# Attention and float8 layer on one core: queries and keys projected three slots ahead of their scores, the float8 product moved within the chunk

## The chip, the core and the metric

The kernel runs on one core of one Trainium2 chip. A core has TensorE (PE; its weight loads are shown apart as PEld), VectorE (DVE), ScalarE (ACT), GpSimd (POOL) and SyncE (SP), which here only issues DMAs. The metric is the device time of one execution in microseconds (us). The kernel before took 2824.32 us, the median of four runs (2822.94 to 2827.62).

## The reference, cut to what matters

The input is x of (4, 1024, 512): four sequences of 1024 tokens. There are 16 heads of 128.

```python
xn = layernorm(x)
q  = rope(rmsnorm(xn @ Wq + bq))            # 16 heads x 128
lk = rope(rmsnorm(xn @ Wlk + blk));  lv = xn @ Wlv + blv
w  = softmax over each 4 tokens of (xn @ Wcmp + bcmp)
entries = sum over the 4 tokens of w * xn   # 256 per sequence
ck = rope(rmsnorm(entries @ Wk + bk));  cv = entries @ Wv + bv
sparse = softmax of the 8 largest q @ ck.T (causal), times cv
local  = softmax of q @ lk.T over a window of 128 back, times lv
out = x + (sparse + local) / 2 @ Wo + bo + fp8(xn) @ fp8(input2)
```

## The kernel before, in words

The 4096 tokens are cut into 32 chunks of 128. A chunk has eight units, a unit is two heads of one chunk, so there are 256 units. All weights stay in SBUF once they are loaded. The main loop (from L785) goes over slots s = -2 to 257. A slot is software-pipelined over several units, and all engines' instructions are written out by hand in the order in which the loop calls them; nothing reorders them. `place(s)` gives the chunk t and the unit u of 0 to 7.

In slot s, for the unit named:

- `scores` (L570 to L581): q times the keys of the previous and the present chunk (lkT) and times the compressed keys (ckT), into PSUM `sc`.
- `weigh` (L603 to L618): VectorE masks, finds the maxima and the eight largest; ScalarE takes exponents. `settle` (L625 to L636) normalises the sparse part, `settle_window` (L641) the window.
- `queries` of unit s + 2 (L443, L444): one product for q and lk of both heads, 128x512 in `qp`.
- `squares`, `spread` (L294, L288, L289): ScalarE sums squares, GpSimd makes the factor `r`. `normalize` (L465, then `rotate`, L307 to L310): VectorE scales into `th`, and VectorE and GpSimd (`rb`) apply the rotation.
- For units from 8 on, `turn_keys` and `fetch_keys` (L510 to L528) turn q and lk: VectorE transposes 32x32 blocks into `thb`, four DMAs write `qk` to DRAM, two DMAs read it back as `qT` and `lkT`. All of these are in SP's queue. Units 0 to 7 are turned by TensorE (`turn_keys_here`, `keep_keys`, L488 to L495).
- `turn` and `fetch` (L659 to L701) do the same for the probabilities of unit s: `probB`, `pr` in DRAM, `probT`.
- `values_of` (L535): lv of unit s + 1, into `vp`; `keep_values` (L547) copies it on ScalarE.
- `values` (L718): context of unit s - 1 from probT, lv and cv. `keep_context` (L733), `to_output` (L751): unit s - 2 into the output.

Work of a chunk is cut into steps of generators, and the loop advances every running generator twice a slot by `steps()`, after `settle` and after `to_output` is called. `chunk_prep(t + 2)` starts at u = 7 and makes the layer norm (`bn_stats` at u = 7, `xn` at 0, transposes `xp` at 1), the compressed entries (`yp` at 2, `ep` at 4, `kv` at 4 to 6) and at u = 7 of the next chunk the transpose `cp` (L410) and VectorE's copy into `ckT` (L412). `chunk_eight(t)` starts at u = 3: three VectorE instructions and four of GpSimd round xn to float8 (L261 to L272), at u = 5 TensorE multiplies (`fp`, L423) and VectorE and GpSimd add the result (`f`, L428, L429).

The PSUM pool tag `pp` has two buffers of 128x512. xp, yp, ep, cp, fp, vp, the transposes of the first units and a few constants share them. The tag `scratch` in SBUF has three buffers for xn, y, qv, qm, f and a mask.

Of the kernel before, what the change touches and what calls it, by code (L numbers as in the profile page):

```python
# [12 lines left out]
F32 = mybir.dt.float32  # L13
# [6 lines left out]
P = 128  # L20
# [4 lines left out]
BLK = 32  # L25
NB = P // BLK
# [12 lines left out]
def kernel(  # L39
# [26 lines left out]
    nc = tc.nc  # L66
# [4 lines left out]
    NU = NH // 2  # L71
    NE = P // RATIO
    NT = B * NCH
    NN = NT * NU
# [3 lines left out]
    work = ctx.enter_context(tc.tile_pool(name="work", bufs=2))  # L78
# [5 lines left out]
        return v.rearrange("p (b i) -> p b i", i=BLK)  # L84

    def scratch(name, shape=(P, 512), dtype=F32):
        return work.tile(list(shape), dtype, tag="scratch", name=name, bufs=3)

    def pp(name):
        return psum.tile([P, 512], F32, tag="pp", name=name, bufs=2)  # L90
# [7 lines left out]
    def load_x(t, purpose):  # L98

        b, c = divmod(t, NCH)  # L100
        xt = work.tile([P, HID], F32, tag="x", name=f"x_{purpose}_{t}")
        nc.sync.dma_start(xt, hidden[b, ts(c, P), :])
        x_tiles[purpose, t] = xt
# [15 lines left out]
    wo_sb = [const.tile([P, 2, HID], F32, name=f"wo_{u}") for u in range(NU)]  # L119

    def load_wqk(u, engine):
        for i, w in enumerate((Wq, Wlk)):
            engine.dma_start(
                wqk_sb[u][:, :, ts(i, 256)], w[:, ts(u, 256)].rearrange("(k p) n -> p k n", p=P)
            )
# [41 lines left out]
    scales = const.tile([P, 2], F32, name="scales")  # L167
# [77 lines left out]
    def late_constants():  # L245

        nc.scalar.dma_start(bo_sb, bo.partition_broadcast(P))
        nc.vector.tensor_tensor(inv, scales[:, 0:1], scales[:, 1:2], ALU.mult)
        nc.vector.reciprocal(inv, inv)

        bp = pp("blvT_ps")
        nc.tensor.transpose(bp[:, 0:NH], blv_n, ident[:NH, :NH])
        nc.scalar.activation(blvT, bp[:, 0:NH], AF.Copy, scale=0.5)

    def quantize(dst, src, scalar, tag):

        v = scratch(f"qv_{tag}") if tag[0] == "x" else src
        m = scratch(f"qm_{tag}")  # L260
        nc.vector.tensor_scalar(v, src, scalar, None, ALU.mult)  # L261
        nc.vector.tensor_scalar(
            m.bitcast(U32), v.bitcast(U32), 0x7F800000, None, ALU.bitwise_and
        )
        nc.vector.tensor_scalar(m, m, FP8_MIN_NORMAL, 1.5 * 2.0**20, ALU.max, ALU.mult)
        nc.gpsimd.tensor_tensor(v, v, m, ALU.add)
        yield
        nc.gpsimd.tensor_tensor(v, v, m, ALU.subtract)
        yield
        nc.gpsimd.tensor_scalar(m, v, FP8_OVERFLOW, 0.0, ALU.mult, ALU.mult)  # L270
        yield
        nc.gpsimd.tensor_tensor(dst, v, m, ALU.add)  # L272
        yield

    w2_sb = const.tile([P, KK, HID], BF16, name="w2_sb")


    w2_raw = [wo_sb[NU // 2 + k][:, 0, :] for k in range(KK)]

    def round_w2():  # L280
        for k in range(KK):
            yield from quantize(w2_sb[:, k, :], w2_raw[k], scales[:, 1:2], f"w2_{k}")

    def rstd_of(ss, n, mul, eps, name):

# [129 lines left out]
    def chunk_eight(t):  # L415

        xt, xnT = x_tiles["sum", t], chunks[t]
        x8 = work.tile([P, KK * P], BF16, tag="x8", name=f"x8_{t}", bufs=1)
        src = xnT.rearrange("p k s -> p (k s)")
        yield from quantize(x8, src, scales[:, 0:1], f"x_{t}")  # L420
        fp = pp(f"fp_{t}")
        for k in range(KK):
            nc.tensor.matmul(  # L423
                fp, x8[:, ts(k, P)], w2_sb[:, k, :], start=(k == 0), stop=(k == KK - 1)
            )
        yield
        f = scratch(f"f_{t}")
        nc.vector.scalar_tensor_tensor(f, fp, inv, bo_sb, ALU.mult, ALU.add)  # L428
        nc.gpsimd.tensor_tensor(xt, xt, f, ALU.add)  # L429
# [4 lines left out]
    def place(n):  # L434

        return divmod(n, NU)
# [41 lines left out]
    def by_dma(n):  # L478

        return NU <= n < NN - 1  # L480
# [15 lines left out]

    def key_tiles(n):
        w = units[n]
        qT = work.tile([P, NB, 2 * BLK], F32, tag="qT", name=f"qT_{n}")
        lkT = work.tile([P, NB, 2 * BLK], F32, tag="lkT", name=f"lkT_{n}", bufs=NU + 2)  # L500
        w["qT"], w["lkT"] = qT.rearrange("p a (i g) -> p (a i) g", g=2), lkT
        return qT, lkT

# [148 lines left out]
    def turn(n):  # L652
        parts = parts_of(n)
        g = len(parts)
        pb = work.tile([P, 1024], F32, tag="probB", name=f"probB_{n}", bufs=1)
        pb = of_heads(pb, n)
        for h in range(2):
            prob = heads.pop((n, h))["prob"]
            nc.vector.transpose(  # L659
                pb[:, :, ds(h * g, g), :],  # L660
                prob[:, parts[0] * P : (parts[-1] + 1) * P].rearrange(
                    "p (g b i) -> p b g i", b=NB, i=BLK
                ),
            )
        turned = dram.tile([P, 1024], F32, tag="pr", name=f"pr_{n}")
        turned = turned[:, 0 : NB * 2 * g * BLK]
        nc.sync.dma_start(turned, pb.rearrange("p b g i -> p (b g i)"))
        units[n]["pr"] = turned
# [27 lines left out]
    def fetch(n):  # L696
        probT = work.tile([P, 1024], F32, tag="probT", name=f"probT_{n}", bufs=1)
        probT = of_heads(probT, n)
        turned = units[n].pop("pr").rearrange("(a j) (b x) -> b j a x", a=NB, b=NB)
        for b in range(NB):  # L700
            nc.sync.dma_start(  # L701
                probT[ds(b * BLK, BLK)].rearrange("j a g i -> j a (g i)"), turned[b]
            )
        units[n]["probT"] = probT
# [61 lines left out]
    def steps(n=1):  # L766
        for g in running:
            for _ in range(n):
                next(g, None)

    def until(g, step):
        for at in g:
            if at == step:
                break

    def for_unit(n, *todo):
        if 0 <= n < NN:
            for f, *more in todo:
                f(n, *more)

    first, rounding = chunk_prep(0), round_w2()
# [4 lines left out]
    pick_tokens()  # L786
    masks()

    for s in range(-2, NN + 2):
        t, u = place(s)  # L790

        if s == -2 or u == 7 and 0 <= t and t + 2 < NT:
            running = [*running[-2:], chunk_prep(t + 2)]
        if u == 3 and 0 <= t < NT:
            load_x(t, "sum")
            running = [*running[-2:], chunk_eight(t)]
        if u == 4 and 0 <= t and t + 2 < NT:
            load_x(t + 2, "norm")

        for_unit(s, (scores, 0), (scores, 1))  # L800
        for_unit(s - 2, (keep_context,))
        for_unit(s, (weigh, 0), (weigh, 1))
        for_unit(s + 2, (queries,))
        if not by_dma(s + 1) and s < NU:
            for_unit(s + 1, (turn_keys_here,))
        for_unit(s, (settle, 0), (settle, 1))
        if s < 0:
            until(first, "B4" if s == -2 else "B6")
        steps()
        for_unit(s + 2, (squares, (0, 1, 2, 3)), (spread,))  # L810
        if not by_dma(s + 1) and s < NU:
            for_unit(s + 1, (keep_keys,))
        for_unit(s, (settle_window, 0), (settle_window, 1))
        for_unit(s - 2, (to_output,))
        steps()
        if by_dma(s):
            turn(s)
        if s == -1:
            until(first, "B7")
        for_unit(s + 1, (values_of,))  # L820
        if s == -1:
            until(first, "B8")
        if not by_dma(s):
            for_unit(s, (turn_here,))
        for_unit(s + 2, (normalize,))
        for_unit(s - 1, (values,))
        if by_dma(s):
            fetch(s)
        else:
            for_unit(s, (keep_turned,))  # L830
        if s + 2 >= NU:
            for_unit(s + 2, (turn_keys,), (fetch_keys,))
        for_unit(s + 1, (keep_values,))
        if s < NU:

            if s == -1:
                late_constants()
                for k in range(KK):
                    nc.scalar.dma_start(w2_raw[k], input2[ts(k, P), :])
            if 0 <= s < KK:  # L840
                for _ in range(4):
                    next(rounding, None)
            if 3 <= s + 5 < NU:
                load_wqk(s + 5, nc.scalar)
            if 3 <= s + 4 < NU:
                load_wlv(s + 4, nc.scalar)
            if 0 <= s + 1 < NU:
                load_wo(s + 1, nc.scalar)
        if u == 6 and 0 <= t and t + 2 < NT:
            load_angles(t + 2)  # L850
        units.pop(s - 1 - NU, None)
# [46 lines left out]
```

## Time and profile before

| | |
|---|---|
| median of four runs | 2824.32 us |
| the profiled execution | 2824.67 us |
| its span, first to last instruction | 2822.9 us |
| granted TensorE clock, mean | 0.998 |
| VectorE busy | 81% |
| ScalarE busy | 46% |
| GpSimd busy | 29% |
| DMA, mean over the span | 142 GB/s |

The page comes from one profiled execution. Busy shares are over the whole span. A group's line names the line of code, the engine, what it writes and reads, the count, the busy time and the mean of one in ns, then the engine's idle time before it and who ended it. In the timeline each row has its start, its length, engine, line and tiles, and rows of the same kind that follow each other are merged. A slot takes 9.0 to 12.7 us, more with later chunks of a sequence (more compressed keys) and in slots with steps of a chunk: the medians in the last chunk of a sequence are 10.92, 11.36, 12.66, 10.92, 11.67, 11.78, 10.92 and 11.29 us for u = 0 to 7.

### The profile page before, as it was taken

To read this page: it belongs to the slowest core of one execution; us is meant where nothing else is said; L and a number is where in the kernel's file an instruction comes from. 1 tells how busy PE (TensorE), PEld (TensorE's weight loads), DVE (VectorE), ACT (ScalarE), POOL (GpSimd) and SP (SyncE) were. 2 spreads that over 40 slices of the span, in tenths; PEclk is the share of its full clock that TensorE was granted. 3 is DMA by queue.
4 is the path that set the end of the run, shared out by engine and by line. 5 is a ranking of instruction groups with operands and counts; after the bars stand their busy time and mean duration, and the time that the engine had idled before them with its cause. 6 is when DMAs were issued, how large, how long until landed. Compare 5 with 4: busy or idle time off the path is not lost. (4 is left out here: it accounts for less than half of the span.)

```text
span 2822.9 us, 48528 instructions
## 1 busy us (share of the span) xinstructions
PE 2769.5 (98%) x12770; PEld 1875.8 (66%) x12969; DVE 2278.4 (81%) x9132; ACT 1300.5 (46%) x5075; POOL 816.6 (29%) x1161
## 2 busy tenths in 40 slices
PE   7999999999999999999999999999999999999998
PEld 4666666666666666666666666666666666666765
DVE  5778888888878888888877788888887777888886
ACT  3444444444444444444444444444444444444443
POOL 3433222322233332232223233222223222322222
PEclk9999999999999999999999999999999999999999
DMA  7344445555444445555544444555554444455554
GB/s 223 95 140 133 135 142 153 149 151 147 137 124 134 139 133 148 149 153 150 148 129 124 136 133 140 150 152 146 152 146 124 132 129 135 136 152 149 150 147 121
DMA packets 620851, 399.85 MB, mean 142 GB/s; under 512 B 306880, under 2 KB 573984, under 8 KB 620576
## 3 DMA queue, kind: packets, MB, share of 16 engines
q1 hardware_dynamic: 608352, 383.18, 48.0%
q10 hardware_dynamic: 12224, 13.56, 1.5%
q8 instruction: 105, 1.72, 0.3%
q14 instruction: 170, 1.39, 0.2%
HBM read 212.53 MB, written 184.03 MB: 140 GB/s over the span
## 5 line engine op out<-in xcount | busy, mean ns | idle before, releaser
L443 PE MATMUL qp<-wqk,xnT 128*128 128x512 f32 x2048 | 944.3, 604 | 3.5 <-DMA scales<-in_L_ffn_scale_dram 2.7
L443 PEld LDWEIGHTS qp<-wqk,xnT 128*128 128x128 f32 x2048 | 370.1, 191 | 383.0 <-issue 369.8
L610 ACT ACTIVATE prob<-sc,neg 128x256 f32<-128x256 f32 (+1 forms) x512 | 235.6, 460 | 791.2 <-DVE taken L609 777.3
L535 PEld LDWEIGHTS vp<-wlv,xnT 128*128 128x128 f32 x2048 | 390.6, 191 | 171.2 <-issue 108.6
L535 PE MATMUL vp<-wlv,xnT 128*128 128x256 f32 x2048 | 487.5, 381 | 7.3 <-DVE lkT L495 4.1
L751 PE MATMUL op<-wo,cT 128*128 128x512 f32 x1024 | 488.1, 599 | 6.0 <-ACT cT L733 1.5
L659 DVE STREAM_TRANSPOSE probB<-prob 128x512 f32<-128x512 f32 (+2 forms) x494 | 282.9, 610 | 76.6 <-ACT prob L641 73.0
L294 ACT ACTIVATE junk<-qp 128x128 bf16<-128x128 f32 x1024 | 283.6, 277 | 96.1 <-remote 53.1
L307 POOL TENSOR_TENSOR rb<-th,cs 128x256 f32<-128x256 f32 x256 | 247.1, 965 | 276.7 <-DVE th L465 276.7
L465 DVE SCALAR_TENSOR_TENSOR th<-qp,r,norm_w 128x128 f32<-128x128 f32 x1024 | 283.1, 339 | 45.8 <-POOL r L289 45.5
L751 PEld LDWEIGHTS op<-wo,cT 128*128 128x128 f32 x1024 | 186.5, 190 | 179.2 <-issue 116.4
L547 ACT COPY lv<-vp 128x256 f32<-128x256 f32 x256 | 95.3, 372 | 450.3 <-PE cp L718 395.7
L288 POOL TENSOR_SCALAR r<-ss 128x4 f32<-128x4 f32 x256 | 49.5, 193 | 861.6 <-ACT junk L294 855.1
L718 PE MATMUL cp<-probT,lv 128*128 128x128 f32 x1920 | 297.5, 275 | 0.6 <-DMA probT<-pr 0.6
L718 PEld LDWEIGHTS cp<-probT,lv 128*128 128x128 f32 x1920 | 274.4, 191 | 14.1 <-PE vp L535 0.9
L289 POOL TENSOR_TENSOR r<-r,nhalf 128x4 f32<-128x4 f32 x256 | 259.6, 1014 | 21.3
L718 PE MATMUL cp<-probT,cv 128*128 128x128 f32 x1536 | 255.1, 275 | 0.0
L580 PE MATMUL sc<-ckT,qT 128*128 128x96 f32 (+7 forms) x1024 | 226.1, 303 | 0.0
L641 ACT ACTIVATE prob<-prob,tot 128x256 f32<-128x256 f32 (+1 forms) x512 | 222.8, 484 | 2.4 <-DVE tot L635 2.4
L309 DVE TENSOR_TENSOR th<-thb,rb 128x128 f32<-128x128 f32 x256 | 87.2, 341 | 158.5 <-POOL rb L307 158.5
L577 PE MATMUL sc<-lkT,qT 128*128 128x128 f32 x1024 | 208.9, 286 | 6.2 <-DMA lkT<-qk 4.4
L718 PEld LDWEIGHTS cp<-probT,cv 128*128 128x128 f32 x1536 | 212.7, 192 | 0.0
(123 smaller groups left out, 4002.6 us busy)
## 6 DMA issues: line engine op xcount, KB each, us to landing
pr<-probB SPq DMA_DIRECT2D x127, 512.0 KB, 2.6
probT<-pr SPq DMA_DIRECT2D x508, 128.0 KB, 2.9
qk<-thb SPq DMA_DIRECT2D x992, 64.0 KB, 2.0
pr<-probB SPq DMA_DIRECT2D x96, 384.0 KB, 2.3
probT<-pr SPq DMA_DIRECT2D x384, 96.0 KB, 2.4
qT<-qk SPq DMA_DIRECT2D x248, 128.0 KB, 2.3
lkT<-qk SPq DMA_DIRECT2D x248, 128.0 KB, 2.6
x_norm<-_attn_hidden_states_dram SPq DMA_DIRECT2D x32, 256.0 KB, 3.0
```

What stands on the lines that cost most here:

```text
L289: nc.gpsimd.tensor_tensor(r, r, nhalf[: ss.shape[0], 0:n], ALU.pow)
L294: nc.scalar.activation(junk[: src.shape[0]], src, AF.Square, accum_out=acc)
L307: nc.gpsimd.tensor_tensor(bb, x12, wide(cs[:, HALF:ROPE]), ALU.mult)
L443: nc.tensor.matmul(qp, xnT[:, k, :], wqk_sb[u][:, k, :], start=(k == 0), stop=False)
L465: nc.vector.scalar_tensor_tensor(th[:, i, :], qp[:, ts(i, D)], r[:, i : i + 1], norm_w[:, i // 2, :], ALU.mult, ALU.mult,)
L535: nc.tensor.matmul(vp[:, 0:256], xnT[:, k, :], wlv_sb[u][:, k, :], start=(k == 0), stop=(k == KK - 1),)
L580: nc.tensor.matmul(sc[:, spa], q, ckT[:, 0:m], start=True, stop=False)
L610: nc.scalar.activation(prob[:, loc], sc[:, loc], AF.Exp, bias=neg[:, 0:1], scale=-1.0, accum_out=tot[:, 0:1],)
L641: nc.scalar.mul(prob[:, loc], prob[:, loc], tot[:, 0:1])
L659: nc.vector.transpose(pb[:, :, ds(h * g, g), :], prob[:, parts[0] * P : (parts[-1] + 1) * P].rearrange("p (g b i) -> p b g i", b=NB, i=BLK),)
L718: nc.tensor.matmul(blocks(cp[:, h, :]), v, probT[:, :, h * len(parts) + i - parts[0], :], start=(i == parts[0]), stop=(i == parts[-1]),)
L751: nc.tensor.matmul(op, cT[:, h, :], wo_sb[u][:, h, :], start=(u == 0 and h == 0), stop=(u == NU - 1 and h == 1),)
```

## The change

- Queries, their squares, factors and normalisation are those of unit s + 3 instead of s + 2; the loop starts at s = -3. TensorE's turning of the first eight units' keys is that of s + 2 instead of s + 1, the turning through DRAM that of s + 3. qT has three buffers, lkT one more. The loads of wqk go out a slot earlier.
- `scratch` has two buffers instead of three. Rounding input2 at the start uses a half of a tile of wo, which is loaded later, as its scratch.
- `chunk_eight(t)` starts at u = 5 instead of 3, so that its product stands at u = 7 instead of 5.

```diff
-        return work.tile(list(shape), dtype, tag="scratch", name=name, bufs=3)
+        return work.tile(list(shape), dtype, tag="scratch", name=name, bufs=2)
...
-    def quantize(dst, src, scalar, tag):
+    def quantize(dst, src, scalar, tag, m=None):
...
-        m = scratch(f"qm_{tag}")
+        if m is None:
+            m = scratch(f"qm_{tag}")
...
-            yield from quantize(w2_sb[:, k, :], w2_raw[k], scales[:, 1:2], f"w2_{k}")
+            spare = wo_sb[NU // 2 + k][:, 1, :]
+            yield from quantize(w2_sb[:, k, :], w2_raw[k], scales[:, 1:2], f"w2_{k}", spare)
...
-        qT = work.tile([P, NB, 2 * BLK], F32, tag="qT", name=f"qT_{n}")
-        lkT = work.tile([P, NB, 2 * BLK], F32, tag="lkT", name=f"lkT_{n}", bufs=NU + 2)
+        qT = work.tile([P, NB, 2 * BLK], F32, tag="qT", name=f"qT_{n}", bufs=3)
+        lkT = work.tile([P, NB, 2 * BLK], F32, tag="lkT", name=f"lkT_{n}", bufs=NU + 3)
...
-    for s in range(-2, NN + 2):
+    for s in range(-3, NN + 2):
...
             load_x(t, "sum")
+        if u == 5 and 0 <= t < NT:
             running = [*running[-2:], chunk_eight(t)]
...
-        for_unit(s + 2, (queries,))
-        if not by_dma(s + 1) and s < NU:
-            for_unit(s + 1, (turn_keys_here,))
+        for_unit(s + 3, (queries,))
+        if s + 2 < NU:
+            for_unit(s + 2, (turn_keys_here,))
...
-            until(first, "B4" if s == -2 else "B6")
+            until(first, ("B3", "B4", "B6")[s + 3])
...
-        for_unit(s + 2, (squares, (0, 1, 2, 3)), (spread,))
-        if not by_dma(s + 1) and s < NU:
-            for_unit(s + 1, (keep_keys,))
+        for_unit(s + 3, (squares, (0, 1, 2, 3)), (spread,))
+        if s + 2 < NU:
+            for_unit(s + 2, (keep_keys,))
...
-        for_unit(s + 2, (normalize,))
+        for_unit(s + 3, (normalize,))
...
-        if s + 2 >= NU:
-            for_unit(s + 2, (turn_keys,), (fetch_keys,))
+        if s + 3 >= NU:
+            for_unit(s + 3, (turn_keys,), (fetch_keys,))
...
-            if 3 <= s + 5 < NU:
-                load_wqk(s + 5, nc.scalar)
+            if 3 <= s + 6 < NU:
+                load_wqk(s + 6, nc.scalar)
```

## The prediction, before the result

> **What bounds the kernel now.** I read the page's engine shares first, then PE's waits, then the timeline around one chunk.
>
> ```profile
> PE 2769.5 (98%) x12770; PEld 1875.8 (66%) x12969; DVE 2278.4 (81%) x9132; ACT 1300.5 (46%) x5075; POOL 816.6 (29%) x1161
> ```
>
> TensorE is busy 98% of the span: 53.4 us of 2822.9 are idle, and some 33 of these lie before the first scores (15.6), in the first and last chunk (7.4 and 5.7) and after the last product (4.1). No edit here removes TensorE work, so a gain can only come out of idle time. The view of PE's waits between 130 and 2780 us (columns: total us, times, longest) says what there is in the middle:
>
> ```profile
> PE sc L577 <- DMA lkT<-qk: 4.4, 6, 1.3
> PE sc L577 <- ACT cT L733: 1.6, 2, 0.8
> PE sc L570 <- DMA qT<-qk: 0.8, 2, 0.4
> PE sc L570 <- ACT cT L733: 0.5, 1, 0.5
> ```
>
> All 11 are score products, 7.3 us in sum. ACT's cT was long done in each, so the DMAs of the turned keys are what came late. In the timeline 5.0 of the 7.3 us stand at the start of slots with u = 5 (slot s: the loop's turn that begins with the scores of unit s; u = s mod 8), two slots behind u = 3, where the float8 product begins. This is what that part does to VectorE in chunk 15 (slot 123 starts at 1371.88, slot 124 at 1382.81; POOL and DVE from two answers of the timeline: start, us, engine, line):
>
> ```profile
> 1379.99 1.27 POOL L266 TENSOR_TENSOR qv_x<-qv_x,qm_x 128x512 f32<-128x512 f32 x1 [7.98 <-DVE row L376]
> 1381.34 0.19 POOL L288 TENSOR_SCALAR r<-ss 128x4 f32<-128x4 f32 x1
> 1381.62 1.01 POOL L289 TENSOR_TENSOR r<-r,nhalf 128x4 f32<-128x4 f32 x1
> 1382.61 1.27 POOL L268 TENSOR_TENSOR qv_x<-qv_x,qm_x 128x512 f32<-128x512 f32 x1
> 1383.87 0.96 POOL L307 TENSOR_TENSOR rb<-th,cs 128x256 f32<-128x256 f32 x1
> 1384.81 0.62 POOL L270 TENSOR_SCALAR qm_x<-qv_x 128x512 f32<-128x512 f32 x1
> ```
>
> ```profile
> 1380.00 1.29 DVE L377 TENSOR_SCALAR spread<-picks,row 128x32 f32<-128x32 f32 x1
> ...
> 1382.67 1.13 DVE L465 SCALAR_TENSOR_TENSOR th<-qp,r,norm_w 128x128 f32<-128x128 f32 x4 [0.16 <-POOL r L289]
> ...
> 1384.87 0.69 DVE L309 TENSOR_TENSOR th<-thb,rb 128x128 f32<-128x128 f32 x1 [0.62 <-POOL rb L307]
> ...
> 1386.49 0.40 DVE L603 CUSTOM_DVE_ANT_0 sc<-sc,mask_b 128x256 f32<-128x256 f32 x1
> ```
>
> POOL's L266 stands ahead of r in its queue, r ahead of VectorE's th, and L268 ahead of rb. So the first softmax instruction of the next slot (L603) comes 3.68 us after slot 124's first score product. I call this distance the **lag**; it was 1.38 in slot 123. Nothing on TensorE waits for it there except, later, keys.
>
> The lag matters at u = 7 (slot 126 starts at 1406.26, slot 127, u = 7, at 1417.18):
>
> ```profile
> 1417.18 0.40 PE L570 MATMUL sc<-lkT,qT 128*128 128x128 f32 x2
> ...
> 1422.96 0.24 PE L410 MATMUL cp<-ident,kv 32*128 32x32 f32 x1
> 1423.14 1.98 PE L751 MATMUL op<-wo,cT 128*128 128x512 f32 x4
> 1424.96 1.89 PE L535 MATMUL vp<-wlv,xnT 128*128 128x256 f32 x8
> ```
>
> ```profile
> 1408.18 0.40 DVE L603 CUSTOM_DVE_ANT_0 sc<-sc,mask_b 128x256 f32<-128x256 f32 x1
> ...
> 1419.27 0.40 DVE L603 CUSTOM_DVE_ANT_0 sc<-sc,mask_b 128x256 f32<-128x256 f32 x1
> ...
> 1425.27 0.16 DVE L412 COPY ckT<-cp 128x32 f32<-128x32 f32 x1
> ```
>
> VectorE ends the copy of ckT at 1425.43, 0.47 us after vp began. Today that is harmless, since vp does not wait for it.
>
> **The change part by part.**
>
> *Keys three slots ahead.* In the steady state each slot keeps its instructions on every engine, SP's queue too: pr, probT, qk, qT and lkT stand in the same order, for a unit one higher. The keys gain a whole slot (10 to 12 us) against waits of at most 1.3, so the 7.3 us go: **-7.3**, between -7.3 and 0. Next in line there is probT: in slot 253 it lands 7.3 us after pr's issue at 2781.09, that is at 2788.4, and cp reads it at 2790.89, so 2.5 us are left.
>
> *Third qT, two scratch buffers, the borrowed half of wo for the weights' rounding.* Cost nothing: two scratch tiles are live at once once the float8 part stands behind y, and the waits that the changed program adds for them (qv_x for xp, qm_x for ep) name products of slots u = 1 and 4, long done at u = 5.
>
> *The float8 product, u = 5 to 7.* Its three VectorE and four POOL instructions move from slots 3 and 4 to 5 and 6, its 0.87 us on TensorE (fp, L423: op starts 0.87 later in slot 125 than in slot 126) and f (0.75 on VectorE) from slot 5 to 7. Slots 3 and 4 lose their delay, which pays nothing but the keys' waits counted above. At u = 7 something new happens. The pool pp has two buffers. There, cp (chunk entries) takes one, fp now the other, and vp is allocated third, into cp's buffer. The changed program's list of waits says so: vp of units 16, 24, ... 248, **30 times, waits for VectorE's ckT copy**; in the kernel before none does. Behind vp stand, on TensorE, the value products and the next slot's scores.
>
> When does that copy end? In chunk 15, step by step:
> - Lag at u = 6 after the change: as in slot 124, 3.68, less 0.40, since L309 took 0.69 instead of 0.29 beside L270, and L270 now stands behind rb_e in the next slot: 3.28. (Losing the 1.29 of spread gains nothing, as th waited for r.)
> - VectorE's turn from L603 to the next L603 in slot 126: 1408.18 to 1419.27 = 11.09. In POOL's queue L270 now stands ahead of r (r ends 0.72 later, th starts 0.66 later) and L272 ahead of rb (0.1): 11.85. The slot is 10.92 long, so the lag at u = 7 is 3.28 + 11.85 - 10.92 = 4.21, instead of 2.09.
> - The copy ended 6.16 after L603, so it ends at 10.37 in the slot; with 0.06 for the semaphore (as from lkT to vp at 42.58), 10.43. TensorE reaches vp at 7.78 + 0.87 = 8.65. Wait: 1.78.
>
> For the other chunks I read the same marks (c is the chunk's place in its sequence, medians, in us from the slot's start). VectorE's turn at u = 6, less its slot, was -0.15, -0.10, -0.24 and 0.02 at c = 2, 3, 6, 7; I take -0.1, so the lag at u = 7 becomes that at u = 4 before, -0.40 - 0.1 + 0.76 = +0.26:
>
> | c | lag u=4 | lag u=7 | ckT end | vp | new wait |
> |---|---|---|---|---|---|
> | 0 | 3.93 | 2.33 | 6.65 | 6.74 | 0.96 |
> | 1 | 3.58 | 1.89 | 6.79 | 7.26 | 0.67 |
> | 2 | 3.74 | 1.89 | 7.00 | 7.32 | 0.98 |
> | 3 | 3.89 | 1.89 | 7.21 | 7.37 | 1.29 |
> | 4 | 3.39 | 1.64 | 7.17 | 7.46 | 0.91 |
> | 5 | 3.49 | 1.64 | 7.38 | 7.57 | 1.11 |
> | 6 | 3.60 | 1.64 | 7.59 | 7.67 | 1.33 |
> | 7 | 3.69 | 1.92 | 8.08 | 7.78 | 1.52 |
>
> Wait = ckT end + (lag u=4 + 0.26 - lag u=7) + 0.06 - vp - 0.87. Four chunks each of c = 1 to 6 (6.29) and three each of 0 and 7 (2.48): 25.2 + 7.4 = **+32.6**. Bounds: a lag 0.7 smaller (kv's arithmetic and r overlapping better) gives 12; VectorE's two kv additions held up by L270 as L309 was, 0.5 more each time, gives 47.
>
> Rule and row on short waits: before, the 2.39 us wait at 75.3 left vp at 1.99 for eight products, the usual 1.89 nearly, while after 2.56 at 40.0 the eight took 3.68. Waits under 1.8, as mine, lie below both. The Trainium skill, "TensorE: Matmul & The Clock Gate", section "HAM oscillation", wants idle gaps kept under some 3.4 us, which the second row undercuts. By that rule my waits cost only themselves; by the 2.56 row taken for every wait, 30 x 1.8 = 54 us more would be due.
>
> On POOL beside VectorE, the row is spread (0.24 alone, 1.29 beside L266, 30 times). The Trainium skill, "SBUF — State Buffer", section "Who interferes with whom", calls this an exclusive lock that a VectorE instruction with two SBUF inputs can lose too; by it the additions of kv beside L270 would be held, which is the sum with 47 instead of 32.6.
>
> *The ends.* A slot is added in front, so one more query product (3.7) is done before the last slots. There, unit 253's softmax has no normalising behind it: pr can go at 10.0 after its scores, probT takes 7.3 (2791.59 to 2798.89), values 1.8, and the scores of unit 255 start at 19.1 instead of 21.3 after those of 253: -2.2. In front, r of unit 0 no longer stands behind lnr (1 us), the product of unit 2 fills waits of tq and vp, and cp of chunk 0 comes later; the loads of wqk leave ACT's queue a slot earlier, with as many bytes a slot as before; I take -1.5. Together **0**, between -4 and +4.
>
> Sum, on the profiled execution's 2824.67 (its span is 2822.9; the median of the four runs, 2824.32, is 0.35 lower): 2824.67 - 7.3 + 32.6 + 0 = **2850**.
>
> **Rivals.**
> 1. *The wait is covered.* VectorE catches up within slot 6, the copy ends before 8.65, and the keys' waits are the whole effect: 2824.67 - 7.3 = 2817. This is the faster side; it holds if the lag at u = 7 stays under some 2.5 us in chunk 15. For it: the lag fell from 3.68 to 1.92 between u = 4 and 6 before. Against: two slots and 0.87 us of fp helped there, here one slot of 10.92 with kv's rotation in it.
> 2. *The lateness runs on.* kv's additions and the slots behind are late too, 47 us or more, and some waits are followed by half-speed products: 2865 to 2890. Against: slot 7 grows by fp and by the wait itself, which gives VectorE 2 to 3 us to recover.
> 3. *A half-covered wait*, 6 to 14 us in sum, which the keys' gain balances: 2820 to 2831.
>
> **How the numbers follow.** Forecast (2831 to 2865) 0.72; covered 0.11; half-covered 0.09; running on 0.08. About 0.2%, 5.6 us, is what a measurement can tell from no change: faster than 2818.7 0.11; within 0.07; slower 0.82. The range takes the forecast's bounds and part of its neighbours: 2826 to 2870.
>
> **What would show it.** In the changed kernel's waits of PE, vp L537 waiting for VectorE some 30 times, 0.7 to 1.8 us each, all at u = 7, and the four key lines gone; lag about 3.3 at u = 6 and 4 at u = 7, back to 1.4 at u = 4. I am wrong if vp's line is missing, if lags at u = 7 stay near 2, or if PE's new idle stands elsewhere, at the ends above all.

## The result, and the profile after

The changed kernel takes 2832.48 us (median of 37 runs, 2829.26 to 2834.91); the kernel before, in the 57 runs by then, 2827.15 (2820.58 to 2835.29). The ratio is 1.0018, 95% interval 1.0014 to 1.0023: slower by 5.3 us, on the edge of what can be told from no change, where the forecast was 25 us. The time lies in the range (2826 to 2870); the size of the change does not lie near the forecast.

The profiled execution of the changed kernel took 2832.96 us (span 2831.0). Its engine shares, from the page, and then the whole of TensorE's waits between 130 and 2780 us (columns: total us, times, longest):

```profile
PE 2769.2 (98%) x12771; PEld 1873.9 (66%) x12969; DVE 2248.6 (79%) x9132; ACT 1296.9 (46%) x5075; POOL 819.7 (29%) x1161
```

```profile
PE vp L537 <- DVE ckT L414: 11.7, 18, 1.1
```

TensorE's work is the same. The four lines of key waits are gone, and the predicted line stands in their place, alone. VectorE is 30 us less busy: spread (L377 before), 1.29 beside POOL's float8 addition, no longer meets it and takes 0.24.

Chunk 15 again, slot 127 (it starts at 1422.94, the next slot at 1436.32), TensorE and VectorE from two answers of the timeline:

```profile
1429.78 1.88 PE L753 MATMUL op<-wo,cT 128*128 128x512 f32 x4
1432.70 1.99 PE L537 MATMUL vp<-wlv,xnT 128*128 128x256 f32 x8 [1.04 <-DVE ckT L414]
```

```profile
1432.49 0.16 DVE L414 COPY ckT<-cp 128x32 f32<-128x32 f32 x1
```

The copy ends at 1432.65 and vp starts 0.05 later. That is 9.71 into the slot; 10.37 was predicted. Where the time went, by TensorE's first score product of a slot, profiled executions against each other:

| stretch | before | after | after less before | predicted |
|---|---|---|---|---|
| to slot 16 | 206.27 | 208.34 | +2.07 | +2.2 |
| slots 16 to 252 | 2563.70 | 2567.65 | +3.95 | +25.3 |
| slot 252 to the last product | 48.80 | 50.95 | +2.15 | -2.2 |

The middle is 21 us below its prediction, the tail 4 above. The waits listed for the middle (11.7 new, 7.3 gone) would make +4.4, close to the +3.95 there. That looks like a settled account; the experiments show that both waits cost more than their lines say.

### The profile page after: what moved, and what is told of

Same layout as the page of the kernel before. It is cut to its first block, busy times and chain, and to the rows that moved or that the text cites. A ratio compares the mean times of both kernels' runs of the same rounds, so it can differ in the third digit from the quotient of the medians.

```text
span 2831.0 us, 48506 instructions
## 1 busy us (share of the span) xinstructions
PE 2769.2 (98%) x12771; PEld 1873.9 (66%) x12969; DVE 2248.6 (79%) x9132; ACT 1296.9 (46%) x5075; POOL 819.7 (29%) x1161
## 3 DMA queue, kind: packets, MB, share of 16 engines
q8 instruction: 105, 1.72, 0.3%
q14 instruction: 169, 1.38, 0.2%
## 5 line engine op out<-in xcount | busy, mean ns | idle before, releaser
L537 PE MATMUL vp<-wlv,xnT 128*128 128x256 f32 x2048 | 487.0, 381 | 17.1 <-DVE ckT L414 11.7
L605 DVE CUSTOM_DVE_ANT_0 sc<-sc,mask_b 128x256 f32<-128x256 f32 (+1 forms) x512 | 203.1, 397 | 7.4 <-PE sc L583 6.7
```

The costliest lines, as they stand in the source:

```text
L537: nc.tensor.matmul(vp[:, 0:256], xnT[:, k, :], wlv_sb[u][:, k, :], start=(k == 0), stop=(k == KK - 1),)
```

## The experiments

The theory after the result, A: the loss is vp's wait for the copy of ckT, the gain of the earlier keys is real, both are small. The rival, B: the wait is only where a slower pipeline shows; taken away, it turns up elsewhere. Each group of runs below had its own runs of the kernel before on the same chip (medians 2827.7, 2828.7, 2829.0 and 2828.0).

**Keys alone.** The float8 product back at u = 3, y in a tile of its own so that the two scratch tiles suffice:

```
-        if u == 5 and 0 <= t < NT:
+        if u == 3 and 0 <= t < NT:
             running = [*running[-2:], chunk_eight(t)]
...
-        y = scratch(f"y_{t}")[:, 0 : 2 * D + 1]
+        y = work.tile([P, 2 * D + 1], F32, tag="y", name=f"y_{t}", bufs=1)
```

> Queries and keys three slots ahead, the float8 product back at u = 3 to 5; y gets a tile of its own, since two scratch buffers would not hold y, qv and qm. Theory A (the change's loss is vp's wait for the ckT copy, 11.7 us in its trace, against 7.2 us of key waits that go, and 4.2 us lost at the two ends): no wait of vp for ckT at u = 7, key waits gone, ends as in the changed kernel: 7.3 off, 4.2 on, so 3 us below the kernel before. Theory B (vp's wait only shows late what TensorE would have waited for anyway, and the loss comes from the deeper pipeline itself): as slow as the changed kernel, 5 us above the kernel before.

2816.52 us, ratio to before 0.9957 (0.9944 to 0.9969). TensorE has no listed wait at all from 130 to 2750 us. The gain is 11 us, not the 3 expected: the keys were worth more than the listed 7.3.

**Float8 alone.** In the kernel before, only the start of chunk_eight moves from u = 3 to u = 5:

> Two slots ahead as before, three scratch buffers, only the float8 product at u = 5 to 7. Theory A: vp waits for ckT 30 times at u = 7, some 12 us in sum; the keys' waits stay and move to slots two behind u = 5, some 7 us; the ends as before: 10 to 13 us above the kernel before, slower than the whole change. The lag at the start of u = 5 is 1.1 to 1.2 us as in the changed kernel. Theory B: 0 to 2 us above the kernel before.

2834.38 us, ratio 1.0022 (1.0013 to 1.0031): 6.7 above, where 10 to 13 was expected. Its waits of PE between 130 and 2750 us:

```profile
PE vp L535 <- DVE ckT L412: 8.9, 15, 1.0
PE sc L577 <- DMA lkT<-qk: 5.1, 9, 1.0
```

The wait of vp comes with the float8 product alone, and the keys' waits stay; they only spread to other slots (now all but u = 3). In slots 16 to 247 the profiled execution is 11.6 longer than that of the kernel before, and 7.8 longer than a second execution of it (below), so part of the miss is the execution that one compares with.

**Float8 one slot earlier**, u = 4 instead of 5 in the changed kernel:

> The changed kernel with the float8 product one slot earlier (u = 4 to 6), so that fp does not meet cp at u = 7. Theory A: no vp wait for ckT, key waits gone, ends as in the changed kernel: 3 us below the kernel before (8 below the changed one). Theory B: 5 us above the kernel before, as the changed kernel.

2816.69 us, ratio 0.9955 (0.9943 to 0.9968), no wait of vp. That is again 11 below the kernel before, not 3.

**cp out of vp's way.** The changed kernel, with the transposed entries written into the free half of the context products' PSUM bank, so that vp no longer inherits their buffer:

```
-        cp = pp(f"cp_{t}")
+        cp = spare_of["ctx"][:, 2 * P :] if t else pp(f"cp_{t}")
...
-        cp = psum.tile([P, 2, P], F32, tag="ctx", name=f"cp_{n}", bufs=1)
+        spare_of["ctx"] = psum.tile([P, 512], F32, tag="ctx", name=f"cp_{n}", bufs=1)
+        cp = spare_of["ctx"][:, 0 : 2 * P].rearrange("p (h d) -> p h d", h=2)
```

> The changed kernel with every instruction in its place; only the transpose cp of the entries writes into the free half of the context's PSUM bank instead of a buffer of pp, so that vp finds a free buffer at u = 7. Theory A: the 18 waits of vp (11.7 us) go and nothing takes their place, as probT has some 2 us left: 3 us below the kernel before. Theory B: TensorE waits as long a little later (cp for probT, or the next scores), 5 us above the kernel before.

2814.85 us, ratio 0.9948 (0.9934 to 0.9962). With the allocation changed and nothing else, 17.6 us go. B falls: nothing took the wait's place. But the sizes fell too. The wait was listed with 11.7 us and its removal gave more. The slots' lengths tell why. Slots 16 to 247 take 2520.0 before, 2524.0 after, 2507.2 in the keys-alone run and 2505.5 here. Against this run, the 29 slots with u = 7 among them are 19.4 us longer in the changed kernel, and of the others only two differ (this run is 0.8 longer there, with a wait for probT); against the keys-alone run the kernel before is 12.8 longer, in 21 slots. Slot 127 of this run (start 1414.30, next slot 1426.36) shows the difference in one slot:

```profile
1421.13 1.88 PE L755 MATMUL op<-wo,cT 128*128 128x512 f32 x4
1422.85 1.89 PE L538 MATMUL vp<-wlv,xnT 128*128 128x256 f32 x8
```

Without a stop, vp begins 0.16 ahead of the end of op (the profile models these ends): successive products overlap in the trace. With the stop it begins 2.92 after op's start instead of 1.72, so 1.20 later, of which the list shows 1.04; and the eight products take 1.99 instead of 1.89. The slot is 1.31 longer. **A stop costs some 0.27 us more than its listed idle time**, and a lateness that stays within the overlap of 0.16 leaves no idle time to list.

**The kernel before once more**, to see whether 12.8 was chance:

> The kernel before, unchanged, for a second profile on the chip of the runs beside it. In its first profile the slots 16 to 248 took 2520.0 us, in e1 (keys three ahead, no wait) 2507.2, which is 12.8 less, though TensorE's waits list only 7.3. Theory A: a stop of TensorE costs its listed wait and some 0.27 us more, since without a stop a product begins about 0.17 us ahead of the modelled end of the one before it, and the first products after a stop are slower; then slots 16 to 248 take 2517 to 2523 here too, with 5 to 9 us of listed waits. Theory B: the 12.8 was the luck of one execution; then less than 2514.

Profiled at 2830.7 us, span 2829.0. Its PE waits between 130 and 2780 us:

```profile
PE sc L577 <- DMA lkT<-qk: 5.6, 9, 1.3
PE sc L570 <- DMA qT<-qk: 1.5, 3, 1.0
PE sc L577 <- ACT cT L733: 1.2, 2, 0.8
PE sc L570 <- ACT cT L733: 1.0, 2, 0.5
```

16 waits, 9.3 listed; slots 16 to 247 are 16.6 longer than those of the keys-alone run (24 slots by more than 0.15). These slots take 2523.8, 0.8 above A's range, so B falls and A's price is rather too low: late keys cost 12.8 and 16.6 in two executions. The same execution's last stretch (from slot 252) took 50.82 instead of 48.80, so the tail of the kernel before is not always shorter than the changed kernel's.

**Why the wait was smaller than predicted.** POOL's L271 (the marking of overflowing values) stands ahead of r in slot 126, and the prediction made VectorE's th wait for r. The changed kernel without it, so that x8 holds other values:

```
-        nc.gpsimd.tensor_scalar(m, v, FP8_OVERFLOW, 0.0, ALU.mult, ALU.mult)
+        if tag[0] != "x":
+            nc.gpsimd.tensor_scalar(m, v, FP8_OVERFLOW, 0.0, ALU.mult, ALU.mult)
```

> The changed kernel without POOL's marking of overflowing values in the chunk's float8 rounding (the 0.62 us instruction that stands ahead of r in slot u = 6); x8 then holds other values. The stops at vp cost 19 us in slots 16 to 248 of the changed kernel. Theory A: r is what VectorE waits for at u = 6, and the chunk entries' additions are held beside that instruction; without it the copy of ckT comes 0.3 to 0.6 us earlier and the stops cost 8 to 14 us less: 2819 to 2825. Theory B: r is not the bound at u = 6, the lag at u = 7 comes from the lag at u = 5 and from the rest of VectorE's work alone: less than 3 us off, 2829 to 2833.

2818.82 us, ratio 0.9964 (0.9950 to 0.9977): 13.7 below the changed kernel, the top of A's gain of 8 to 14; the slots 16 to 247 are 12.7 shorter. First slot 126 of the changed kernel (start 1412.03; VectorE, then POOL), then VectorE and POOL in this run's slot 126 (start 1406.39) and its copy of ckT in slot 127 (start 1417.31):

```profile
1415.11 0.40 DVE L605 CUSTOM_DVE_ANT_0 sc<-sc,mask_b 128x256 f32<-128x256 f32 x1
...
1421.10 0.59 DVE L311 TENSOR_TENSOR kv<-ra_e,rb_e 32x32 f32<-32x32 f32 x1 [0.23 <-POOL rb_e L309]
...
1423.06 1.13 DVE L467 SCALAR_TENSOR_TENSOR th<-qp,r,norm_w 128x128 f32<-128x128 f32 x4
```

```profile
1421.04 0.61 POOL L271 TENSOR_SCALAR qm_x<-qv_x 128x512 f32<-128x512 f32 x1
...
1422.01 1.02 POOL L291 TENSOR_TENSOR r<-r,nhalf 128x4 f32<-128x4 f32 x1
```

```profile
1415.47 0.18 DVE L312 TENSOR_TENSOR kv<-ra_e,rb_e 32x32 f32<-32x32 f32 x1 [0.23 <-POOL rb_e L310]
...
1416.90 1.07 DVE L468 SCALAR_TENSOR_TENSOR th<-qp,r,norm_w 128x128 f32<-128x128 f32 x4
...
1426.28 0.16 DVE L415 COPY ckT<-cp 128x32 f32<-128x32 f32 x1
```

```profile
1415.80 1.01 POOL L292 TENSOR_TENSOR r<-r,nhalf 128x4 f32<-128x4 f32 x1
```

kv's first addition takes 0.59 beside L271 and 0.18 without it: 0.41. The copy of ckT comes 0.58 earlier in slot 127 (it ends at 9.13 instead of 9.71), so 0.17 is left, and that is r's. r ends 0.58 earlier (10.42 in the slot instead of 11.00). In the changed kernel VectorE is busy with kv and the two probB transposes until 10.97, and th starts at 11.03, just behind r; without L271 th starts at 10.51, 0.06 ahead of the modelled end of the transposes, and its four instructions take 1.07 instead of 1.13. So L271 does make the lateness, as theory A has it, and in both of A's ways: 0.41 by holding the addition, some 0.17 by standing ahead of r.

The Trainium skill, "SBUF — State Buffer", section "Who interferes with whom", says that a VectorE instruction with two SBUF inputs contends with a POOL instruction that reads SBUF. The two rows of kv agree.

**The price of a later copy.** One VectorE instruction (128x480, measured 0.70) that nothing needs, ahead of each copy of ckT in the changed kernel:

```
+        if t >= 2:
+            nc.vector.scalar_tensor_tensor(
+                cp[:, NE:512], bo_sb[:, NE:512], inv, bo_sb[:, NE:512], ALU.mult, ALU.add
+            )
         nc.vector.tensor_copy(ckT[:, ts(c, NE)], cp[:, 0:NE])
```

> The changed kernel with one more VectorE instruction that nothing needs, 128x480, directly ahead of each copy of ckT from chunk 2 on; by the row of f (0.74 us for 128x512) it takes 0.70. Theory A: behind vp's wait nothing hides, so each of the 30 stops grows by what the copy is later, 0.70, or by less where TensorE came last until now (c = 1, 2 and 4): 13 to 20 us in slots 16 to 248, a time of 2845 to 2853. Theory B: VectorE or the next slot takes the lateness up: less than 6 us. As to TensorE's clock: the longest stops become 1.8 us; if a stop of that length halves the speed, the eight vp products behind it take 3.7 us instead of 2.0, and the time goes beyond 2860.

2853.68 us, ratio 1.0088 (1.0071 to 1.0105): 21.2 above the changed kernel, just above A's range. In slots 16 to 247, 29 slots with u = 7 are each 0.67 to 0.77 longer (21.7 in sum) and all others equal. No chunk had slack left. Against the cp run these 29 slots are 41.1 longer with 33.3 of listed idle time, 0.27 a stop again. Its waits of PE:

```profile
PE vp L541 <- DVE ckT L418: 33.8, 30, 1.8
```

The longest stop, 1.80, left the granted clock at 1.00 and vp at 1.99, so no stop here started a slow stretch.

**The tail.** In slot 254 of the changed kernel TensorE waits for probT, and then runs at half its speed (a granted clock of 0.50 from 2802.4, still in the wait, to 2809.2):

```profile
2797.99 1.89 PE L537 MATMUL vp<-wlv,xnT 128*128 128x256 f32 x8
2804.23 1.19 PE L720 MATMUL cp<-probT,lv 128*128 128x128 f32 x4 [4.35 <-DMA probT<-pr]
2805.22 1.06 PE L720 MATMUL cp<-probT,cv 128*128 128x128 f32 x4
...
2807.78 0.63 PE L572 MATMUL sc<-lkT,qT 128*128 128x128 f32 x2
```

Is it the wait, the clock, or neither that sets the end? Three edits of the cp run. First, eight products into an unused query buffer, placed in that wait of slot 254, which nothing reads; then four of them:

> e4 (no wait of vp) with eight products of 128x512 that nothing reads (about 3.9 us), put into TensorE's 4.35 us wait for probT in slot 254. Theory A: the half-speed stretch after that wait (1.06 us for four context products instead of 0.61, from 2804 to 2809 in the changed kernel's profile) comes from the idle time and costs 2.5 to 4 us at the end; filled, the time falls from 2814.9 to 2811 to 2812.5. Theory B: the tail is set by VectorE's softmax and the DMA of probT, and TensorE's speed there is covered: within 1 us of e4.

> e4 with four idle products instead of e7's eight: those took 7.03 us (each stands as two in the records), 2.3 more than the wait of 4.35, so that the context products behind them began 2.3 late, and the end still came 1.5 us earlier. Theory A (the half-speed stretches behind the wait cost 3.5 to 4 us): four products take 3.5, the wait is filled but for 0.8, nothing is late, and the time is 2810.5 to 2812, 3 to 4 below e4. Theory B (the clock is worth no more than the 1.6 of e7, the late products having been covered): 2812.5 to 2814.

Eight took 7.03 us, not the 3.9 that I had put, and made the context products late: 2813.28 (ratio 0.9944, 0.9932 to 0.9957), 1.6 below the cp run, between the two theories. Four took 3.60: 2811.16 (0.9940, 0.9926 to 0.9953), 3.7 below, as A had it, though single executions of the two runs just overlap (2809.48 to 2811.99 against 2811.45 to 2816.07). There the context products behind the rest of the wait (0.92) take 0.68 and 0.61, and from slot 252 to the end it is 48.63 us instead of 50.73, which is 2.1 of the 3.7. Then the last unit's query product, with all that follows from it, two slots ahead as in the kernel before, the others three ahead:

```
+        q = s + 3 if s + 3 < NN - 1 else NN - 1 if s + 2 == NN - 1 else NN
...
-        for_unit(s + 3, (queries,))
+        for_unit(q, (queries,))
...
-        for_unit(s + 3, (squares, (0, 1, 2, 3)), (spread,))
+        for_unit(q, (squares, (0, 1, 2, 3)), (spread,))
...
-        for_unit(s + 3, (normalize,))
+        for_unit(q, (normalize,))
...
-            for_unit(s + 3, (turn_keys,), (fetch_keys,))
+            for_unit(q, (turn_keys,), (fetch_keys,))
```

> e4 with the last unit's query product, squares, normalising and turned keys two slots ahead as in the kernel before; all other units three ahead. The 4.35 us wait for probT in slot 254 is then covered by a query product of 3.7 us, and the tail should fall from 39.8 to about 38 us as before. Theory A (the emptied slot 253 costs the tail 2 us): 2812.5 to 2813.5. Theory B (the softmax of the last units sets the end either way, as the prediction had it, which gave the emptied slot a gain of 2.2): 2815 to 2818.

2809.48 us, ratio 0.9930 (0.9917 to 0.9944), better than both theories said, and the lowest median of all: 46.37 us from slot 252 to the end. Slot 252 is now the one without a query product (7.50 long instead of 10.92), and the product of 3.68 lies in slot 253, between the scores of unit 253 and the use of its probT in slot 254, which no longer waits. What is left is one wait ahead of slot 255:

```profile
2784.52 0.77 PE L573 MATMUL sc<-lkT,qT 128*128 128x128 f32 x2 [2.12 <-ACT cT L737]
```

Behind it the clock was 0.50 again, from 2784.4 to 2787.8. Two idle products there:

> e8 (last query product two ahead) with two idle products, 1.75 us, in its wait of 2.12 us ahead of the scores of slot 255, which then ran at a granted clock of 0.50 for 3 us. Theory A (the clock falls for the idle time and delays what follows): full speed there and 1 to 2 us less than e8: 2807.5 to 2808.5. Theory B (the scores are followed by waits for VectorE and ScalarE, which cover it): 2809 to 2810.

2810.64 us (0.9939, 0.9927 to 0.9951): no gain in time, though the scores ran at full speed (0.60 instead of 1.06 for the longest) and the profiled tail is 0.8 shorter (45.56). The medians can't price this edit: the two runs stand in different groups, their executions overlap (2808.45 to 2812.02 against 2808.34 to 2810.41), and the profiled execution here reaches slot 16 at 210.65, the one of the run before at 208.05, which is 2.6 lost ahead of anything that the edit touches. So neither theory is shown; what the traces show is the 0.8 of the tail.

## Why the prediction was wrong, by its steps

**Keys three ahead: -7.3, "between -7.3 and 0".** The direction was right, the bound was not: -12.8 against the profiled execution and -16.6 against the second. The step took TensorE's list of waits for the price of the waits. A listed wait leaves out the overlap of successive products (0.16) and the slower products after it (0.1), the list names fewer waits than there are late slots (11 against 21), and one execution's DMA waits are not another's (7.3 and 9.3 listed, in other slots). A view of the profile before could have warned of it: each slot's length against the shortest of its kind (same chunk place and u) gives 9.7 us for slots 16 to 247.

**The wait of vp: +32.6, between 12 and 47.** The mechanism was right: which instruction waits for which, at u = 7, with nothing to hide it. The size was 19.4, in 29 slots. In chunk 15:

| term | predicted | measured |
|---|---|---|
| lag at u = 6 | 3.28 | 3.08 |
| VectorE's turn at u = 6 | 11.85 | 11.38 |
| lag at u = 7 | 4.21 | 3.54 |
| ckT's end in the slot | 10.37 | 9.71 |
| slot longer by | 1.78 | 1.31 |

The first term was 0.20 too large: the rounding now begins from a lag of 1.13 at u = 5; it was 1.38 at u = 3. The second was mis-sized more. To the 11.09 of the kernel before it added 0.66 for r's lateness and 0.1 for rb. Measured, r added some 0.17, since VectorE was itself busy until 0.03 before r came, and rb nothing (VectorE waits 0.62 for it in both kernels). What did come was the hold-up of kv, 0.41 a time, which I had kept for the upper bound of 47. And 0.29 went off, which I had not looked for: in slot 126 of the kernel before VectorE waited 0.52 for rb_e, in the changed kernel 0.23. Together 11.09 + 0.17 + 0.41 - 0.29 = 11.38. The row of before:

```profile
1414.47 0.18 DVE L309 TENSOR_TENSOR kv<-ra_e,rb_e 32x32 f32<-32x32 f32 x1 [0.52 <-POOL rb_e L307]
```

The rule for the other chunks (the lag at u = 4 before plus 0.26) inherited both errors and overstated all but one: at c = 4 it gave 3.65, and 2.78 was measured; only c = 0 came out, 4.19 and 4.12. One error went the other way: a stop costs 0.27 more than its idle time, in the 29 slots up to 7.8 us, which no term of mine held.

**The ends: 0.** The start came out, +2.07 for +2.2, in part by luck: the 1.5 in it was an assumption, and slot 16 starts at 208.05 to 210.65 in the ten profiled runs with the keys three ahead. The tail was wrong: +2.15 for -2.2 (against the second execution of before, +0.1; the keys-alone run, with the same emptied slot 253, took 49.28). As far as probT the step was right: the values behind it begin 17.3 after the scores of 253 (2786.91 to 2804.23), and 10.0 + 7.3 was predicted. It then put the values at 1.8 and all that follows the scores of 255 at no change, and did not ask at what speed TensorE runs once the 3.7 of query product that covered the wait is gone. At the granted clock of 0.50 the values took 3.55, so the scores of 255 come 20.9 after those of 253, not 19.1; with four idle products in the wait they come at 19.2. From the scores of 255 to the last product it is 19.16 instead of 16.60, with the clock at 0.50 again from 2816.1 to 2819.4; in the run with eight idle products, at 1.00 through this stretch, it is 16.87. The runs with four idle products and with the last query product two ahead take 2.1 and 4.4 us off the tail of the cp run.

**The sum.** +2.1 at the start, +19.4 for vp, -12.8 to -16.6 for the keys, -2.6 for the place of fp itself (a slot with fp is 0.86 longer at u = 5 and 0.77 at u = 7, in 29 chunks; I had taken 0.87 for both), +0.1 to +2.2 in the tail: +2.4 to +8.3, by which of the two executions of before is taken, against 5.3 between the medians. The two large terms nearly cancel. That comes near the arithmetic of the third rival, a wait of 6 to 14 us which the keys' gain balances, but it is not its mechanism: nothing was half covered, every stop was paid in full, as the later copy showed.

## What to carry to other kernels

Price a stop by the length of its stretch against the same stretch without it, in more than one execution; the list of waits finds the place and understates the price. When a change takes one more buffer of a rotating pool, look up who gets that buffer next and whose last reader it then waits for: here one PSUM allocation undid the gain of the whole change, and moving it away gives 0.9948, with the last query product 0.9930. If the queue of a bottleneck engine is emptied near the end, see which wait lay under the removed work, and at what clock the engine comes out of it.

## What the runs showed of the hardware

TensorE's clock did not follow the length of a single wait. After 1.80 us it stayed at 1.00, after 2.12 and 4.35 it was 0.50, after 2.39 in the kernel before the eight vp products still took 1.99, and in the run with four idle products two waits of 0.92 and 0.96 with 0.66 of transposes between them were followed by 0.50 from 2794.1 to 2797.5. The same two waits in the run with two idle products, 0.92 and 0.96, were not: the context products behind them took 0.61.

The granted clocks of the 13 traces show what does. In every trace the stretches of 0.50 up to the last product begin and end on a grid with steps of 3.41 us, and where the grid lies differs from one execution to the next. From 50 us on the clock fell to 0.50 fifteen times, each time behind a step in which TensorE was busy for at most 1.72 of the 3.41 us, about half. Of all the other steps at full clock in that time only two had so little (1.62 and 1.70). So a wait counts by how much idle time falls into one step:

| wait | run | TensorE busy in the steps that it falls into | clock behind |
|---|---|---|---|
| 2.39 | the kernel before | 1.88 and 2.56 | 1.00 |
| 2.12 | last query product two ahead | 1.40 and 3.32 | 0.50 |
| 1.80 (slot 127) | later copy | 3.28 and 1.74 | 1.00 |
| 0.92 and 0.96 | four idle products | 1.53, both in one step | 0.50 |
| 0.92 and 0.96 | two idle products | 2.41 and 2.41 | 1.00 |

By these rows the 1.80 came close to a slow stretch.

The Trainium skill, "TensorE: Matmul & The Clock Gate", section "HAM oscillation", wants idle gaps of TensorE no longer than about 3.4 us; the 2.12 here, and the two short waits close together, fell under that and lost the speed all the same.
